# A decoder layer with a mixture of experts on one core: four whole expert tiles placed beside the cross attention's last chunk and the sort

## The chip, the cores and the metric

The kernel runs on one core of a Trainium2 chip. The metric is the time of one execution in device microseconds (us). Five engines work side by side, each through its own list of instructions in order: TensorE (PE; PEld is its weight load), VectorE (DVE), ScalarE (ACT), GpSimd (POOL) and SyncE (SP), which here only issues transfers. An instruction waits on semaphores for what it needs, and everything behind it on its engine waits with it.

## The reference, cut to what matters

`x` holds 2 x 1024 tokens of 256 numbers. Three blocks follow each other, each on a normalized copy of `x`, each added to `x`:

```python
x = x + self_attention(layernorm(x))         # 16 heads of 16, softmax plus a bias, then a layernorm
x = x + cross_attention(layernorm(x), ctx)   # 16 heads, 77 context tokens, masked
x = x + moe(layernorm(x))

def moe(flat):                               # 2048 tokens, 8 experts, hidden size 1024
    probs = softmax(flat @ gate_W)
    topk_w, topk_idx = top_k(probs, 2)       # every token goes to two experts
    combine = one_hot(topk_idx) weighted by topk_w / sum(topk_w)
    out = 0.5 * gelu(flat @ shared_W + shared_b)
    for e in range(8):
        h = gelu(flat @ W1[e] + b1[e])
        out = out + combine[:, e] * (h @ W2[e] + b2[e])
    return layernorm(out) * gamma + beta
```

Everything is float32. The kernel computes the experts only for the tokens that chose them: 4096 pairs of a token and an expert, sorted by expert.

## The kernel before, in words

The tokens are worked on in chunks of 512 (four chunks, `c` = 0 to 3) or in tiles of 128 (`i` = 0 to 15). `xs` holds `x`, 128 tokens by 16 tiles by 256. Up to some 475 us the self attention runs as a stream of products of scores (L549, L595), a maximum on VectorE (L556), an exponential on ScalarE (L603) and products with the values (L612).

From there until the sort is done, the order on PE, DVE, ACT and POOL is written out by hand: the string `todo` (L1124 to L1158) is a list of words, and each word calls one function, which issues its instructions on their engines in that order. The words for one tile of the cross attention are:

- `scores` (L681, PE: four products into four PSUM banks), `masked` (DVE: L696 four times, then the maximum L700), `less` (POOL, L705: subtracts the maximum, 128x1232), `exps` (ACT, L708), `sums` (DVE: L712 and L713), `shares` (POOL, L718: times the reciprocal, 128x1232);
- `turn` (L720: 16 transposes on PE, four copies on ACT into `PT`), and for each chunk `attend` (L731, two words) and `output` (L748, two words: products on PE, and L761 on DVE adds to `xs`).

After `output` a chunk is normalized for the experts: `stats` and `dev` (`measure`, and `norm_scale` at L134: L137 adds eps on DVE, L138 takes the power -0.5 on POOL), `off` (`offsets`, L167: L173 on DVE; the norm ahead of the cross attention multiplies by `live` first, L171), `norm` (four activations at L184, then the rows are written to `xnd` in DRAM), `flip` (transposes into `xnT`), `gate` (logits). `shared` are the products of the shared layer.

The sort follows when the gates are there, in three groups (chunks 0 and 1; 2; 3): `choose` takes the two best experts by a dozen small operations on DVE, `rank` counts on PE how many earlier pairs have the same expert, `place` makes slot numbers, `hots` (L881, L888) and `invert` (PE) turn the list around, `filled` adds the groups' parts. When all four chunks are in, `totals` and `owners` find for every tile of pairs its expert, `pick` and `rows` give for every slot the row to be gathered (`from_row`) and the row to be scattered to (`to_row`), and `biases` takes the tiles' biases.

An expert tile is then either 256 pairs (the first `NP` = 12) or 128 pairs (11 in this run). For each: POOL gathers its rows from `xnd` (L1466, an indirect transfer), PE transposes them (L1482) and DVE copies them into `xgT` (L1490), PE multiplies by the expert's first matrix (L1496), ACT applies gelu (L1503), PE multiplies by the second matrix (L1515), DVE adds the bias (`y`, L1522), POOL scatters `y` to `pairs` in DRAM (L1526). The weights, 1 MB for each of the two matrices, come by SP (L1384, L1389) into four sets of buffers, three tiles ahead. The order of this part is made by a scheduler. A last stage sums each token's two rows with the shared layer, normalizes and writes out.

Of the kernel before, what the change touches and what calls it, by code (L numbers as in the profile page):

```python
# [8 lines left out]
F32 = mybir.dt.float32  # L9
# [5 lines left out]
P = 128  # L15
# [18 lines left out]
NTE = NP + NS - 2 * NP  # L34
EB = N // P
# [5 lines left out]
def decoder_kernel(  # L41
# [92 lines left out]
    def norm_scale(mv, n, eps):  # L134

        r = small.tile([P, 4], F32, tag="rstd", name="rstd")
        nc.vector.tensor_scalar(r[:, :n], mv[:, :, 1], eps, None, ALU.add)  # L137
        nc.gpsimd.tensor_tensor(r[:, :n], r[:, :n], nhalf[:, :n], ALU.pow)  # L138
        return r
# [27 lines left out]
    def offsets(c, live=None, dst=None):  # L167

        mv, r = moments.pop(c)[1], tokens[c]
        if live is not None:  # L170
            nc.vector.tensor_tensor(r[:, :4], r[:, :4], live, ALU.mult)  # L171
        off = small.tile([P, 4], F32, tag="off", name=f"off{c}")
        nc.vector.scalar_tensor_tensor(off, mv[:, :, 0], -1.0, r[:, :4], ALU.mult, ALU.mult)  # L173
        if dst is None:
            dst = work.tile([P, 4, D], F32, tag="xn", name="xn")
        tokens[c] = r, off, dst
# [74 lines left out]
    for _ in range(30):  # L251
        nc.tensor.matmul(idle[:, :P], lhsT=ident, rhs=ident, start=True, stop=True)  # L252
# [406 lines left out]
    PTs, oTs = {}, {}  # L659
# [60 lines left out]
    def turn(i):  # L720
        c, t = i // 4, i % 4
        if c not in PTs:
            PTs[c] = cr2.tile([P, H, 512], F32, tag="PT", name=f"PT{c}")
        st = sts[i % 4]
        for k in range(4):
            pp = one("ppT").rearrange("p (h f) -> p h f", f=P)
            for h in range(4):
                nc.tensor.transpose(pp[:T2, h, :], st[:, 4 * k + h, :], ident)  # L728
            nc.scalar.copy(PTs[c][:T2, 4 * k : 4 * k + 4, P * t : P * t + P], pp[:T2, :, :])  # L729

    def attend(c, G):  # L731
        b, PT = c // 2, PTs[c]
        if c not in oTs:
            oTs[c] = cr2.tile([P, 2, 512], F32, tag="oT", name=f"oT{c}")
        po = one("pco")
        for i in range(2):
            for r in range(4):
                h = 8 * G + 2 * r + i
                nc.tensor.matmul(
                    po[32 * r : 32 * r + 32, :],  # L740
                    lhsT=vx[:T2, b, h, :, :].rearrange("p i d -> p (i d)"),
                    rhs=PT[:T2, h, :],
                    start=(i == 0),
                    stop=(i == 1),
                )
        nc.scalar.copy(oTs[c][:, G, :], po)

    def output(c, u):  # L748

        pu = one("pu").rearrange("p (t f) -> p t f", f=D)  # L750
        for t in range(2):
            for G in range(2):
                nc.tensor.matmul(
                    pu[:, t, :],
                    lhsT=oTs[c][:, G, P * (2 * u + t) : P * (2 * u + t) + P],
# [4 lines left out]
        x2 = xs[:, 4 * c + 2 * u : 4 * c + 2 * u + 2, :]  # L760
# [320 lines left out]
    def o_gamma(h):  # L1081
        c, o = out_of(h)
        mv = moments.pop(("o", c))[1]
# [12 lines left out]
    def exps_b(m):  # L1096
# [29 lines left out]
        exps_b:122 times_v:121:1 collect:14 exps_b:123 times_v:122:1 o_stats:14  # L1126
        exps_b:124 times_v:123:0 scores:0 o_dev:14 exps_b:125 masked:0 times_v:124:0
        exps_b:126 times_v:125:0 exps_b:127 times_v:126:0 o_gamma:14 scores:1 masked:1
        less:1 scores:2 masked:2 o_add:14 times_v:127:0 less:0 collect:15 exps:1
        q_stats:2 q_dev:2 o_stats:15 exps:0 o_dev:15 sums:0 o_gamma:15 q_off:2 less:2  # L1130
        sums:1 exps:2 o_add:15 sums:2 shares:0 q_norm:2 q_stats:3 close shares:1
        q_flip:2:1 add_bu:2 shares:2 scores:3 masked:3 q_flip:2:0 turn:0 less:3 scores:4
        q_dev:3 exps:3 masked:4 turn:1 sums:3 less:4 shares:3 scores:5 exps:4 masked:5
        turn:2 sums:4 query:2:1 query:2:0 less:5 shares:4 constant:0 scores:6 exps:5
        masked:6 turn:3 sums:5 less:6 shares:5 constant:1 scores:7 exps:6 attend:0:0
        masked:7 attend:0:1 turn:4 sums:6 q_off:3 less:7 shares:6 constant:2 scores:8
        q_norm:3 exps:7 masked:8 output:0:1 stats:0:1 output:0:0 q_flip:3:1 add_bu:3
        turn:5 sums:7 less:8 shares:7 constant:3 scores:9 q_flip:3:0 exps:8 masked:9
        turn:6 sums:8 less:9 shares:8 constant:4 scores:10 query:3:0 exps:9 masked:10
        query:3:1 turn:7 sums:9 less:10 shares:9 constant:5 scores:11 stats:0:0 exps:10  # L1140
        attend:1:0 masked:11 dev:0 attend:1:1 turn:8 sums:10 off:0 less:11 norm:0
        shares:10 constant:6 scores:12 exps:11 masked:12 output:1:1 stats:1:1 output:1:0
        turn:9 sums:11 less:12 shares:11 constant:7 scores:13 exps:12 masked:13
        flip:0:1:0 flip:0:0:0 turn:10 sums:12 gate:0 less:13 shares:12 constant:8
        scores:14 exps:13 masked:14 turn:11 sums:13 less:14 shares:13 constant:9
        scores:15 stats:1:0 exps:14 attend:2:0 masked:15 dev:1 attend:2:1 turn:12
        sums:14 off:1 less:15 norm:1 shares:14 exps:15 output:2:1 output:2:0 turn:13
        sums:15 shares:15 stats:2:1 flip:1:1:0 stats:2:0 flip:1:0:0 turn:14 dev:2 gate:1
        choose:0 earlier:1 turn:15 attend:3:0 attend:3:1 off:2 rank:0 place:0 output:3:0
        stats:3:0 output:3:1 norm:2 stats:3:1 dev:3 flip:2:1:0 flip:2:0:0 shared:0:0  # L1150
        hots:0:0 off:3 hots:1:0 norm:3 gate:2 hots:0:1 flip:3:1:1 choose:1 flip:3:0:0
        shared:1:1 gate:3 shared:3:0 rank:1 earlier:2 invert:0 choose:2 place:1 hots:2:0
        rank:2 hots:2:1 totals shared:3:1 hots:1:1 invert:1 place:2 hots:3:0 shared:0:1
        hots:3:1 filled:0 invert:3 owners invert:2 shared:2:0 filled:1 weights filled:2
        filled:3 pick shared:2:1 rows biases shared:1:0
# [34 lines left out]

    constants = []
# [10 lines left out]
    def zeros():  # L1202
        nc.gpsimd.memset(euler, 2.718281828459045)
        for t in (nta, ntb, twos, share2):
# [8 lines left out]
    slot_no = number("slot_no", [[1, NS]], 0, 0, [P, NS])  # L1213

    pair_no = number("pair_no", [[N, 2], [P, NT]], 2 * N, 1, [P, 2, NT])
    constants += [lambda: nc.gpsimd.memset(ones, 1.0), triangle, zeros]

    crossing = ExitStack()
    cr2 = crossing.enter_context(tc.tile_pool(name="cr2", bufs=2))
    cr1 = crossing.enter_context(tc.tile_pool(name="cr1", bufs=2))  # L1220
# [3 lines left out]
    filled_to = rt.tile([P, E, EB], F32, name="filled_to")  # L1224
# [22 lines left out]
    def owners():  # L1247
        nc.vector.tensor_tensor(
            filled_to,
# [7 lines left out]
        nc.vector.tensor_scalar(spare[:, 1, :], nta[:, 0, 4:], -1.0, float(EB), ALU.mult, ALU.add)  # L1257
        src, dst = nta, ntb
        for k in (1, 2, 4):
# [7 lines left out]
            twos[:, 1:], src[:, 1, 4:], 2.0, float(2 * NP), ALU.mult, ALU.min  # L1267
# [4 lines left out]
        for ts, to, no in (  # L1272
            (slice(0, NP), twos[:, 1:], slot_no[:, 0 : 2 * NP : 2]),
# [9 lines left out]
        nc.vector.tensor_reduce(owner, past, AX.X, ALU.add)  # L1283
        nc.vector.tensor_scalar(owner, owner, float(E - 1), None, ALU.min)
        nc.vector.tensor_copy(owner_i, owner)


        nc.vector.tensor_scalar(
            spare[:, 0, :], share2[:, :E], -1.0, float(EB), ALU.mult, ALU.add
        )  # L1290
        nc.vector.tensor_tensor(spare[:, 1, :], spare[:, 1, :], share2[:, 1:], ALU.add)
        for k, ts in enumerate((slice(0, NP), slice(NP, NTE))):
# [6 lines left out]
        nc.vector.tensor_reduce(skipped, over, AX.X, ALU.add)  # L1299
        nc.vector.tensor_tensor(  # L1300
            column[:, : 2 * NP].rearrange("p (i k) -> p i k", k=2),
            slot_no[:, : 2 * NP].rearrange("p (i k) -> p i k", k=2),
            skipped[:, :NP].unsqueeze(2).to_broadcast([P, NP, 2]),
# [3 lines left out]
            column[:, 2 * NP :], slot_no[:, : NTE - NP], share2[:, 0:1], skipped[:, NP:],  # L1307
            ALU.add, ALU.add,
        )
        nc.vector.tensor_scalar(pick, column, row_no[:, 0:1], None, ALU.is_equal)  # L1310
        nc.vector.tensor_copy(count_i, ends[:, E - 1 : E])

    def pick_columns():
        held["ppk"] = one("ppk")[:, :NS]
        nc.tensor.matmul(held["ppk"], lhsT=places, rhs=pick, start=True, stop=True)

    def rows():

        nc.vector.tensor_copy(pair, held["ppk"])
        nc.vector.tensor_scalar(from_row, pair, N - 1, None, ALU.bitwise_and)  # L1320
        nc.vector.tensor_scalar(to_row, pair, 2 * N, None, ALU.bitwise_xor)

    def biases():

        nc.vector.tensor_scalar(mine, owner[:E, :], row_no[:E, 0:1], None, ALU.is_equal)
        pb1 = one("pb1")[:, : NTE * NH].rearrange("p (i h) -> p i h", h=NH)
        for h in range(NH):
            nc.tensor.matmul(
                pb1[:, :, h], lhsT=b1[:, h * P : (h + 1) * P], rhs=mine, start=True, stop=True
            )  # L1330
        nc.vector.tensor_copy(b1s, pb1)
# [22 lines left out]
        pick=pick_columns,  # L1354
        rows=rows,
        biases=biases,
# [9 lines left out]
    w1s = [wmoe.tile([P, 2, HID], F32, name=f"w1_{k}") for k in range(3)]  # L1366
# [371 lines left out]
```

## Time and profile before

| | us |
|---|---|
| median of 3 runs (977.98 to 978.78) | 978.05 |
| the profiled execution's own time | 986.99 |
| its span, first to last instruction | 985.3 |
| self attention's last products with values end (PE) | 501.8 |
| tile 15's `sums` (L712) begin | 609.2 |
| first gather of expert rows begins (POOL) | 668.8 |
| first products of an expert begin (PE, L1496) | 676.3 |
| first expert tile's `y` (L1522) | 700.7 |
| last stage's first sums (L1615) | 955.1 |

In the windows of the profile each column behind an engine's busy time is its number of instructions; PEclk is the clock that TensorE was granted, 1.00 being full speed. A busy PE is an upper bound: its products are pipelined and their ends are modelled, so the spacing of the starts tells more than the sum of durations. In the timeline a row gives start, duration, engine, line, what is written from what, and in brackets the idle time before it and what ended it.

### The profile page before, as it was taken

The numbers are of one execution on the slowest core, as the hardware profiler recorded it, in microseconds if no ns is written. First come the engines' busy times: TensorE is split into PE (matmuls) and PEld (weight loads), VectorE is DVE, ScalarE is ACT, GpSimd is POOL, SyncE is SP. The second block draws the span as 40 slices with busy tenths as digits, with TensorE's granted clock in tenths as the row PEclk, the third lists the DMA queues.
The fourth block names the chain that finished last, engine by engine and source line by source line (L and its number), as shares of the span: only waits on it lengthen the run. The fifth ranks groups of instructions, "written<-read, shape, count | busy, mean of one in ns | idle before, by whom it ended". The sixth has DMA issues, their size and how long they took to land.

```text
span 985.3 us, 16174 instructions
## 1 busy us (share of the span) xinstructions
PE 922.7 (94%) x6080; PEld 542.9 (55%) x6080; DVE 579.4 (59%) x1172; ACT 544.1 (55%) x1079; POOL 403.5 (41%) x344
## 2 busy tenths in 40 slices
PE   9999999999999999999947999998999999999983
PEld 6543433333333333333315667686878878888762
DVE  5874668878888797987589998471111031011117
ACT  4566767877878788887844777313332322234312
POOL 1642323553335564343566887005243432122103
PEclk9999999999999999999976999689999999999997
DMA  7300000000000000000000000007854654699343
GB/s 172 59 1 2 2 2 1 2 1 1 2 1 2 1 2 1 1 1 1 1 0 18 1 23 22 27 17 264 307 196 156 206 180 153 206 308 329 132 145 125
DMA packets 65162, 75.62 MB, mean 77 GB/s; under 512 B 17967, under 2 KB 57036, under 8 KB 65076
## 3 DMA queue, kind: packets, MB, share of 16 engines
q1 hardware_dynamic: 59604, 63.62, 20.0%
q0 software_dynamic: 3360, 8.79, 2.4%
q10 hardware_dynamic: 2112, 2.10, 0.6%
q8 instruction: 50, 0.82, 0.4%
q14 instruction: 36, 0.29, 0.1%
HBM read 66.10 MB, written 8.78 MB: 76 GB/s over the span
## 4 chain that ended last, share of the span: by engine, by line
PE 72%; DVE 15%; DMA 9%; issue 2%; ACT 1%; POOL 1%; SPq 0%; DVEq 0%; POOLq 0%; ACTq 0%
PE sA L549 14%; PE av L612 13%; PE sB L595 11%; PE po L1515 9%; PE ph L1496 9%; DMA pairs<-y,to_row 7%; PE pp L502 3%; PE pb L394 2%; PE pv L340 1%; DVE cm L700 1%; DVE cs L712 1%; PE pq L664 1%; DVE scrap L696 1%; PE idle L252 1%; DVE xs L1094 1%
## 5 line engine op out<-in xcount | busy, mean ns | idle before, releaser
L556 DVE TENSOR_REDUCE mx<-sA 128x1 f32<-128x512 f32 x512 | 317.4, 683 | 95.4 <-PE sB L595 88.4
L603 ACT ACTIVATE pt<-sB 128x512 f32<-128x512 f32 x512 | 264.8, 603 | 63.1 <-PE sB L595 63.0
L549 PE MATMUL sA<-kT,scrap 32*128 32x512 f32 x1024 | 253.8, 619 | 0.0
L595 PE MATMUL sB<-qB,kT 32*128 32x512 f32 x1024 | 247.6, 616 | 0.0
L625 POOL TENSOR_TENSOR avs<-avs,part 128x512 f32<-128x512 f32 x112 | 142.1, 1269 | 231.0 <-ACT part L624 225.7
L1503 ACT ACTIVATE hT<-ph,b1s 128x256 f32<-128x256 f32 (+1 forms) x184 | 77.7, 424 | 184.6 <-PE ph L1496 179.7
L549 PEld LDWEIGHTS sA<-kT,scrap 32*128 32x128 f32 x1024 | 100.4, 183 | 82.3 <-ACT pt L603 54.5
L612 PE MATMUL av<-pt,vaug 128*32 128x512 f32 x1024 | 137.4, 605 | 3.2 <-DVE mx L556 3.2
L595 PEld LDWEIGHTS sB<-qB,kT 32*128 32x128 f32 x1024 | 97.7, 183 | 37.9 <-issue 30.1
L1522 DVE TENSOR_TENSOR y<-po,b 128x512 f32<-128x512 f32 (+1 forms) x23 | 13.0, 564 | 176.4 <-PE po L1515 169.7
L1496 PE MATMUL ph<-xgT,w 128*128 128x256 f32 (+1 forms) x576 | 109.3, 334 | 1.3 <-DMA w<-in_L_ffn_W_dram 0.7
L1515 PE MATMUL po<-w,hT 128*128 128x256 f32 x432 | 105.2, 382 | 3.4 <-DVE y L1522 3.3
L1496 PEld LDWEIGHTS ph<-xgT,w 128*128 128x128 f32 x576 | 91.3, 191 | 21.4 <-ACT hT L1503 7.5
L1515 PEld LDWEIGHTS po<-w,hT 128*128 128x128 f32 x432 | 77.7, 190 | 14.4 <-DVE y L1522 5.5
L1526 POOL DMA_INDIRECT pairs<-y,to_row x35 | 35.3, 1007 | 115.1 <-DMA pairs<-y,to_row 79.4
L1466 POOL DMA_INDIRECT xg<-xnd,from_row x35 | 34.3, 979 | 104.5 <-PE px L1482 64.2
L612 PEld LDWEIGHTS av<-pt,vaug 128*32 128x32 f32 x1024 | 21.0, 109 | 100.4 <-DVE mx L556 91.4
L624 ACT COPY part<-av 128x512 f32<-128x512 f32 x108 | 65.7, 609 | 5.4 <-PE av L612 5.1
L138 POOL TENSOR_TENSOR rstd<-rstd,nhalf 128x4 f32<-128x4 f32 x20 | 21.7, 1084 | 71.2 <-DVE rstd L137 70.8
L729 ACT COPY PT<-ppT 77x512 f32<-77x512 f32 x64 | 32.7, 588 | 2.2 <-PE ppT L728 1.5
L1515 PE MATMUL po<-xnT,hT 128*128 128x256 f32 x128 | 31.8, 383 | 1.9 <-DVE y L1522 1.9
L194 PE MATMUL pxT<-ident,xn 128*128 128x128 f32 x96 | 17.5, 305 | 16.7 <-ACT xn L184 16.6
(262 smaller groups left out, 1137.9 us busy)
## 6 DMA issues: line engine op xcount, KB each, us to landing
w<-in_L_ffn_W_dram SPq DMA_DIRECT2D x36, 1024.0 KB
xnT<-in_L_ffn_W_dram SPq DMA_DIRECT2D x10, 1024.0 KB
b<-in_L_ffn_b_dram SPq DMA_DIRECT2D x23, 128.0 KB
xs<-in_x_dram SPq DMA_DIRECT2D x4, 512.0 KB
xnd<-xn SPq DMA_DIRECT2D x4, 512.0 KB
w<-pairs SPq DMA_DIRECT2D x3, 512.0 KB
w<-pairs ACTq DMA_DIRECT2D x3, 512.0 KB
out_dram<-scrap SPq DMA_DIRECT2D x3, 512.0 KB
```

What stands on the lines that cost most here:

```text
L549: nc.tensor.matmul(s, lhsT=units[h // 4, "q"][r0 : r0 + 32, q0 : q0 + P], rhs=units[h // 4, "k", g % 2][r0 : r0 + 32, 512 * kh : 512 * kh ...
L556: nc.vector.tensor_reduce(largest[h][:, qt, hh : hh + 1, kh], s, AX.X, ALU.max)
L595: nc.tensor.matmul(s, lhsT=units[h // 4, "k", g % 2][r0 : r0 + 32, kt * P : (kt + 1) * P], rhs=shifted[h][r0 : r0 + 32, :], start=True, st ...
L603: nc.scalar.activation(powers[m, hh], s, AF.Exp, scale=1.0 / 16.0)
L612: nc.tensor.matmul(av[32 * hh : 32 * hh + 32, :], lhsT=vaug[:, kt, 4 * g + hh, :, b], rhs=powers.pop((m, hh)), start=True, stop=True,)
L624: copy(part, av)
L625: nc.gpsimd.tensor_tensor(sums[h], sums[h], part, ALU.add)
L1466: fetched[i] = nc.gpsimd.indirect_dma_start(out=xg[:, s, :], out_offset=None, in_=xnd[:, :], in_offset=bass.IndirectOffsetOnAxis(ap=from_r ...
L1496: nc.tensor.matmul(ph[:, hc % group, :], lhsT=w1[:, kc, hc * P : (hc + 1) * P], rhs=xgT[:, kc, :], start=(kc == 0), stop=(kc == 1),)
L1503: hidden[i] = nc.scalar.activation(hT[:, hc, :], ph[:, hc % group, :], AF.Gelu, bias=b1s[:, i, hc : hc + 1])
L1515: nc.tensor.matmul(po[:, s, :], lhsT=hT[:, hc, s * P : (s + 1) * P], rhs=w2[:, hc, :], start=(hc == 0), stop=(hc == NH - 1),)
L1526: nc.gpsimd.indirect_dma_start(out=pairs[:, :], out_offset=bass.IndirectOffsetOnAxis(ap=to_row[:, k : k + 1], axis=0), in_=y[:, s, :], in_ ...
```

## The change: what it does, and the diff

Of the 12 tiles with 256 pairs, four (`NE`) are made out of the first three chunks alone. When group 1 is sorted, `counts` and `full` find four whole tiles among the experts' pairs so far, `pick_full`, `rows_full` and `biases_full` do for them what `pick`, `rows` and `biases` do for all, and `used` takes them off the later count. Their parts (`load`, `fetch`, `spread`, `first`, `second`) stand as words in `todo` beside the last chunk's words; eight tiles of 256 and the 11 of 128 remain for the loop. `first` is a quarter of the first layer, `second` half of the second. For this the sort's groups 0 and 1 are moved ahead, between the words of tiles 11 to 15. `turn`, `attend` and `output` work on pairs of tiles, 256 tokens, in place of chunks; the products and copies for a chunk stay the same in number of columns. The norm's addition of eps, the product with `live` and the offset (now two instructions) are issued on POOL. At the start 27 in place of 30 products keep PE busy. The weights of tiles 0 and 2 lie in half of `xnT` and a buffer of their own, those of 1 and 3 in the buffer of `PT`. SP's list, in the built order: the rows of chunks 0 to 2, the loads of tiles 0 and 1, the rows of chunk 3, the first matrix of tile 2, its second, the first matrix of tile 3, then some sixteen loads of owners into registers, and behind them the second matrix of tile 3 and the loads of tiles 4 and on.

```diff
     def norm_scale(mv, n, eps):
         r = small.tile([P, 4], F32, tag="rstd", name="rstd")
-        nc.vector.tensor_scalar(r[:, :n], mv[:, :, 1], eps, None, ALU.add)
+        nc.gpsimd.tensor_scalar(r[:, :n], mv[:, :, 1], eps, None, ALU.add)
         nc.gpsimd.tensor_tensor(r[:, :n], r[:, :n], nhalf[:, :n], ALU.pow)
...
         if live is not None:
-            nc.vector.tensor_tensor(r[:, :4], r[:, :4], live, ALU.mult)
+            nc.gpsimd.tensor_tensor(r[:, :4], r[:, :4], live, ALU.mult)
         off = small.tile([P, 4], F32, tag="off", name=f"off{c}")
-        nc.vector.scalar_tensor_tensor(off, mv[:, :, 0], -1.0, r[:, :4], ALU.mult, ALU.mult)
+        nc.gpsimd.tensor_tensor(off, mv[:, :, 0], r[:, :4], ALU.mult)
+        nc.gpsimd.tensor_scalar(off, off, -1.0, None, ALU.mult)
...
-    for _ in range(30):
+    for _ in range(27):
         nc.tensor.matmul(idle[:, :P], lhsT=ident, rhs=ident, start=True, stop=True)
...
     todo = """
...
+        gate:1 choose:0
+        turn:11 less:13 shares:12 scores:14 attend:5 exps:13 masked:14 sums:13 rank:0
+        place:0 output:5 earlier:1 stats:2:1 hots:1:0 turn:12 hots:0:1 less:14 shares:13
+        dev:2 scores:15 off:2 exps:14 shared:1:1 masked:15 sums:14 norm:2 shared:1:0
+        flip:2:1:0 flip:2:0:0 gate:2 shared:2:0 turn:13 hots:0:0 choose:1 less:15
+        shared:2:1 shares:14 rank:1 invert:0 earlier:2 exps:15 hots:1:1 sums:15 attend:6
+        counts filled:0 invert:1 place:1 hots:2:1 turn:14 hots:2:0 shares:15 invert:2
+        full shared:0:0 load:0 filled:1 filled:2 pick_full rows_full output:6 turn:15
+        biases_full attend:7 fetch:0 used fetch:1 spread:0 fetch:2 output:7 stats:3:0
+        stats:3:1 dev:3 load:1 first:0:0 off:3 norm:3 first:0:1 first:0:2 first:0:3
+        spread:1 fetch:3 flip:3:0:1 flip:3:1:0 first:1:0 first:1:1 second:0:0 second:0:1
+        load:2 gate:3 first:1:2 first:1:3 choose:2 spread:2 totals rank:2 place:2
+        hots:3:1 hots:3:0 first:2:0 second:1:0 shared:3:0 invert:3 owners first:2:1
+        filled:3 pick second:1:1 load:3 first:2:2 rows first:2:3 spread:3 second:2:0
+        first:3:0 biases first:3:1 first:3:2 first:3:3 second:3:0 weights second:2:1
+        second:3:1 shared:3:1
     """.split()
...
+    def full_tiles():
+        nc.vector.tensor_tensor(
+            full_to,
+            held["pce"].unsqueeze(2).to_broadcast([P, E, NFULL]),
+            bounds.unsqueeze(1).to_broadcast([P, E, NFULL]),
+            ALU.is_ge,
+        )
+        nc.vector.tensor_reduce(fta[:, 4:], full_to, AX.X, ALU.add)
+        src, dst = fta, ftb
+        for k in (1, 2, 4):
+            nc.vector.tensor_tensor(dst[:, 4:], src[:, 4:], src[:, 4 - k : 4 - k + E], ALU.add)
+            src, dst = dst, src
...
+    def set_of(i):
+        return i % 2 if i < NE else (i - NE + 2) % 4
...
+    def fetch_first(i):
+        for s in range(2):
+            gather(2 * i + s, xgs[i % 2], s, N - N // 4)
+
+    def turn_first(i):
+        px = one("px").rearrange("p (kc f) -> p kc f", kc=2)
+        for kc in range(2):
+            for s in range(2):
+                nc.tensor.transpose(
+                    px[:, kc, s * P : (s + 1) * P], xgs[i % 2][:, s, kc * P : (kc + 1) * P], ident
+                )
+        nc.vector.tensor_copy(xgTs[0], px)
+
+    def first_part(i, q):
+        ph = one("ph").rearrange("p (h f) -> p h f", h=2)
+        for j in range(2):
+            hc = 2 * q + j
+            for kc in range(2):
+                nc.tensor.matmul(
+                    ph[:, j, :],
+                    lhsT=weights[i][0][:, kc, hc * P : (hc + 1) * P],
+                    rhs=xgTs[0][:, kc, :],
+                    start=(kc == 0),
+                    stop=(kc == 1),
+                )
+            nc.scalar.activation(
+                hTs[i % 2][:, hc, :], ph[:, j, :], AF.Gelu, bias=b1s[:, i, hc : hc + 1]
+            )
+
+    def second_part(i, s):
+        w2, b2 = weights[i][1]
+        if s == 0:
+            held["po2", i] = one("po2").rearrange("p (s f) -> p s f", s=2)
+        po, y = held["po2", i], ys[i % 2]
+        for hc in range(NH):
+            nc.tensor.matmul(
...
+        if s == 0:
+            return
+        nc.vector.tensor_tensor(y, po, b2.unsqueeze(1).to_broadcast([P, 2, D]), ALU.add)
+        for s in range(2):
+            scatter(2 * i + s, y, s)
...
-        got = {0: fetch(0)}
-        gate_in = nc.sync.dma_start(out=landed, in_=xgs[0][0:1, :, 0:1])
-        got[1] = fetch(1)
+        got = {NE: fetch(NE)}
+        gate_in = nc.sync.dma_start(out=landed, in_=xgs[NE % 3][0:1, :, 0:1])
+        got[NE + 1] = fetch(NE + 1)
         with tc.issue_after(gate_in.ins):
-            second_of_0()
-            weights[1] = fetch_weights(1)
-            weights[2] = fetch_weights(2)
+            weights[NE + 1] = fetch_weights(NE + 1)
+            weights[NE + 2] = fetch_weights(NE + 2)
...
-        behind = tiles((0, 2), always + 2, got, None)
-        behind = tiles((2, always), always + 2, got, behind)
+        behind = tiles((NE, NE + 2), always + 2, got, None)
+        behind = tiles((NE + 2, always), always + 2, got, behind)
```

## The prediction

> **What bounds the kernel now.** I read the slices first.
>
> ```profile
> PE   9999999999999999999947999998999999999983
> DVE  5874668878888797987589998471111031011117
> POOL 1642323553335564343566887005243432122103
> PEclk9999999999999999999976999689999999999997
> ```
>
> One slice is 24.6 us. Up to slice 20 PE is full and DVE has room. In slices 20 to 25 DVE is full: cross attention. In 25 to 27 nobody is full and PE's clock drops: the sort. From 28 on PE is full and DVE idle: the expert tiles. So four tiles can be had for less than they cost only if they fill holes that DVE, or the low clock, makes in PE's time between 500 and 680 us. The windows of that stretch:
>
> ```profile
> 560.00:580.00 20.00, 19.19 (x133) 11.89 (x133) 19.59 (x35) 15.14 (x26) 17.71 (x15) 1.00 0.01 1
> 580.00:600.00 20.00, 20.00 (x152) 14.94 (x154) 19.59 (x37) 14.49 (x25) 17.04 (x12) 1.00 0.08 27
> ...
> 616.00:633.00 17.00, 17.00 (x68) 9.84 (x67) 4.73 (x20) 3.93 (x8) 0.00 (x0) 0.52 0.10 32
> ```
>
> After the window's length come PE, PEld, DVE, ACT and POOL, then the clock. DVE has 19.59 of 20 us, and POOL 17 to 18. In the third PE seems full, but at clock 0.52, with 68 products in 17 us. The timeline shows why DVE is full:
>
> ```profile
> 554.06 2.25 POOL L705 TENSOR_TENSOR st<-st,cm 128x1232 f32<-128x1232 f32 x1
> ...
> 555.08 1.25 DVE L171 TENSOR_TENSOR rstd<-rstd,live 128x4 f32<-128x4 f32 x1
> 556.26 2.25 POOL L718 TENSOR_TENSOR scrap<-scrap,cs 128x1232 f32<-128x1232 f32 x1
> 556.36 2.17 DVE L173 SCALAR_TENSOR_TENSOR off<-bnmv,rstd 128x4 f32<-128x4 f32 x1
> ```
>
> Operations on four columns, 0.15 us elsewhere, end just when POOL's product ends (556.31, 558.51): with SBUF inputs DVE waits for POOL. L700 and L712 keep their 1.43 us beside POOL. The chain of waits, too, goes mostly through DVE's L696, L700 and L712 from 499 to 609. Last, the loop's pace:
>
> ```profile
> 700.69 0.69 DVE L1522 TENSOR_TENSOR y<-po,b 128x512 f32<-128x512 f32 x1 [4.76 <-PE po L1515]
> ...
> 715.64 0.69 DVE L1522 TENSOR_TENSOR y<-po,b 128x512 f32<-128x512 f32 x1 [3.59 <-PE po L1515]
> ```
>
> A tile of 256 costs 14.95 us of the path, PE without holes.
>
> **The sum.** What follows the loop's first `y` is 985.3 - 700.7 = 284.6 us, and loses 4 x 14.95 = 59.8. So the change wins if that `y` comes less than 59.8 us later than 700.7. I build that time from two stretches.
>
> **Stretch one, paced by DVE,** from tile 1's `masked` (L696 at 498.9) until the early tiles' `from_row` is written. DVE's work in the new order, with before's rows:
> - 15 `masked` (1.53 + 1.44) and 16 `sums` (1.43 + 0.21): 44.6 + 26.2 = 70.8
> - two output norms (2.1 of statistics, L1085 2.74, L1094 4.09, waits for POOL included): 17.8
> - five chunk norms' statistics, 2.1 each: 10.5; six L761 of 0.66 and a `collect`: 4.7
> - the sort of groups 0 and 1: `choose` 3.1 + 2.6, `place` 1.6 + 1.4, six `hots` of 1.64 (0.68 + 4 x 0.27, overlapping), 9.8 in all, copies, `earlier` and `filled` 2.0, `full` 15 small operations at 0.2, 3.0, and rows 0.5: 24.0
>
> Together 127.8. Before did 97.9 of such work between 498.9 and the end of tile 15's `sums` (610.8), in 111.9 us: 14 us over. Of these L171 and L173 took 6.4 (1.25 + 2.17 + 1.81 + 1.80, less 4 x 0.16); they go, as the change puts them on POOL. The other 7.6 are waits for PE or ACT; I keep 7.
>
> New is that the sort's small operations with SBUF inputs stand between tiles 11 and 15, where POOL is busy. At five places (`choose:0`, `place:0`, `hots:1:0`, `hots:0:0`, `place:1`) a `shares` or `dev`/`off` has just become ready. Bounds: 0, if DVE slips in ahead, to 20 us, eight 2.25 us products of POOL left there and 2 us of a norm. I take 2.0 for each of the five, near the 1.25 to 2.17 of the rows above: 10. So 498.9 + 127.8 + 7 + 10 = **643.7**. PE's own work here, 112 us by the spacing of the rows (`scores` 1.24, `turn` 1.82, `attend` and `output` 1.8, `query` 1.75, `shared` and `gate` 1.85), fits beneath.
>
> The norms' 19 instructions on POOL in this stretch have no row. Bounds: 0.13 to 0.19 (IOTA, CAST of few columns) and 1.0 (L138, a power). I take 0.2, nearest in kind: 4 us among 94 of POOL's, in 145. That hides; at 1.0 it fits still, and only chunk 2's norm, on which group 1 waits, would come 3 us later. They read statistics from DVE as L137 and L173 did, and ACT's L184 waits behind them, as before. At the kernel's end two L137 of 1.25 and 1.19 us vanish from DVE, but the addition then queues behind the same product on POOL: 0, between 0 and -2.
>
> **Stretch two, paced by PE.** After `from_row` PE still has `output` 1.8, `turn` 1.9, the biases 2.0, `attend` 1.8, the transposes 0.6, `output` 1.8 = 9.9. That covers the gather: before, 5.7 us from from_row's last operation (667.9) to L1482 (673.6). It covers the first weights: the owner is known some 2 us before 643.7, its register load took 1.2 (owner_i written at 664.3, load issued at 665.4), and 1 MB with another ahead 9.1 (677.35 to 686.5): 652. First expert product: 653.6. From there four tiles and the last chunk: first layers 4 x 7.1, second 4 x 7.0, three transposes 1.8, `flip` 1.1, `gate` 1.85, `totals` 1.4, `rank` 1.3, two `shared` 3.8, `invert` 2.0, `pick` 0.4, biases 2.0 = 72.0, so 725.6. DVE has only some 25 us of work in this stretch; chunk 3's sort waits for PE, not the reverse. Then the loop: transposes and copy 1.6, two first layers 14.2, one second 7.0: 748.4.
>
> Hops between engines: 3.5 us (seven turns of `spread` or of gelu before a product, 0.5 each, as L1522 to L1515's 0.35 or L1503's 0.39). Clock: before ran 27 us of 606 to 681 at about half, costing some 13.7 us of PE; bounds 0 and 13.7. I take two stretches of 3.4 us, the length of the three short drops, 3.4 lost, because PE is fuller: **755.3**. The scatters of two tiles (7 us apart each) fall into stretch two on POOL; nothing on PE waits for them before `y` of the loop's second tile, 15 us later. Three idle products fewer at the start (0.16 us each, two instructions per product, 1.0): the transposes follow at 11.12 but their input is ready at 10.35; gain 0.6.
>
> Sum: 755.3 - 700.7 - 59.8 - 0.6 = **-5.8 us** against the profiled run, 986.99 to 981.2. The runs shown have a median 978.05, 8.9 below it; the difference carried over gives 972.2.
>
> The Trainium skill speaks against one piece: "SBUF — State Buffer", in "A bandwidth-pool intuition that's wrong", says that a transfer issued by GpSimd waits for its descriptors while DVE holds the shared port, some 620 ns becoming some 3100. No row before shows it: L1466 took 0.95 to 1.22 us with DVE nearly idle, and in the changed kernel gathers run beside the sort. By that rule the first tile's two gathers would come an estimated 5 us later, and the sum would be near -1.
>
> **Rivals.**
> 1. *Everything fits* (0.20): DVE is let in ahead of POOL (-7), no clock drop (-3.4), hops hidden (-2): -18, 960. For it: PE's holes close as work fills them. Against: waits in every stretch of the trace.
> 2. *DVE shut out by POOL* (0.26), slower: place, group 0 and 1's sort among tiles 11 to 15; price up to 10 us more, and while PE waits for `taken` and `place` its clock falls, which costs up to 10 more. It decides once `from_row` comes 6.4 us later than 643.7, after 650.1. Likeliest 11 us over, +5: 983, at most 992. For it: 0.52 of the clock in exactly these words before. That the holes aren't there at all, PE being "9" in the slices, ends here too.
> 3. *Late weights* (0.09): the second matrix of tile 3 waits behind some sixteen register loads on SP after `owners`. Between 0 and the 1.2 us above for each, up to 19 us, with some 20 us of PE work over it; 6 us may show: 978, no change.
> 4. *Forecast* (0.45).
>
> **Numbers.** 972.2. Range 960 to 986: rival 1's value below, most of rival 2 above; about 2 in 10 stay out. One measurement tells 0.2%, 2 us, from no change. Faster 0.65 (forecast and rival 1), same 0.09, slower 0.26.
>
> **What would show it.** `from_row` of the early tiles near 644, first L1496-like product near 654, first `y` of the loop near 755, then 14.95 us a tile. In the words around `choose` and `hots`, DVE operations whose ends match POOL's ends, some 2 us at five places. PEclk at 0.5 for two stretches only between 600 and 690. Wrong if `from_row` comes after 650, if PE waits for weights, or if a POOL instruction of four columns takes 1 us.

## The result, and the profile after

The changed kernel takes 1005.03 us (median of 4 runs, 1001.54 to 1008.06) against 978.41 of the kernel before beside it: a ratio of 1.0262, interval 1.0217 to 1.0306. It is slower by 26.6 us, where 5.8 us less were predicted. Its profiled execution took 1003.7 us with a span of 1002.0.

The slices of the changed kernel (one is 25.05 us), to lay beside those of before:

```profile
PE   9999999999999999999929998978999999989973
DVE  5774668877887887968598888612301141011107
POOL 2732323553345664443477974211214431145104
PEclk9999999999999999999969997969999999999997
```

Counted from 0, as in the prediction: DVE is less full in slices 20 to 24 (9, 8, 8, 8, 8 for 8, 9, 9, 9, 8), and the first expert products now stand in slice 26. But there PE has 7 and its clock 6, and in slice 27 PE has 8: holes, where before's expert tiles ran at 9 (from slice 28 on). The windows there (window's length, PE, PEld, DVE, ACT, POOL, clock, DMA share, GB/s):

```profile
650.00:660.00 10.00, 8.48 (x56) 6.13 (x56) 3.87 (x15) 2.49 (x4) 2.34 (x3) 0.83 1.05 350
660.00:670.00 10.00, 5.39 (x14) 3.61 (x13) 0.12 (x1) 3.70 (x8) 1.73 (x4) 0.68 0.29 101
670.00:680.00 10.00, 8.87 (x31) 6.72 (x30) 1.38 (x2) 2.48 (x5) 2.05 (x2) 0.64 0.35 114
```

Between 660 and 670 PE issues 14 rows of products (against 56 in the window before), and neither DVE, ACT, POOL nor the DMA is busy for more than 3.7 of the 10 us: they wait for each other. The timeline of PE shows for what (start, duration, line, in brackets the idle time before it):

```profile
657.09 1.03 PE L1503 MATMUL ph<-xgT,xnT 128*128 128x256 f32 x4
658.68 1.99 PE L1503 MATMUL ph<-xgT,xnT 128*128 128x256 f32 x8 [0.56 <-ACT hT L1510]
664.72 3.78 PE L1503 MATMUL ph<-xgT,xnT 128*128 128x256 f32 x8 [4.04 <-ACT hT L1510]
669.06 3.78 PE L1503 MATMUL ph<-xgT,xnT 128*128 128x256 f32 x8 [0.56 <-ACT hT L1510]
673.41 2.08 PE L1503 MATMUL ph<-xgT,xnT 128*128 128x256 f32 x4 [0.56 <-ACT hT L1510]
```

Four rows of products make one group, and a part is two groups, for two blocks of 128 hidden columns. After every first group PE stands 0.56 to 0.62 us until ACT's gelu (L1510) has read it. Once it stands 4.04 us, and then eight rows take 3.78 us instead of 1.99: half the clock. ACT's own row for the 4.04 is `norm:3`, four scalings that wait for POOL's offset and have the next gelu behind them:

```profile
662.23 2.07 ACT L189 ACTIVATE xn<-xs,off,rstd 128x256 f32<-128x256 f32 x4 [1.91 <-POOL off L178]
664.21 0.45 ACT L1510 ACTIVATE hT<-ph,b1s 128x256 f32<-128x256 f32 x1
```

The waits of PE between 650 and 775 us (in total, times, longest) put nearly all of it in one line, and no wait for weights is among them (the 0.6 put down to "issue" stands at the same place of a part, 727.5, so it is probably the sixteenth wait of this kind):

```profile
PE ph L1503 <- ACT hT L1510: 12.4, 15, 4.0
PE px L1493 <- DMA xg<-xnd,from_row: 1.0, 2, 0.6
PE px L1662 <- ACT scrap L929: 0.7, 1, 0.7
PE ph L1503 <- issue: 0.6, 1, 0.6
PE ph L1676 <- DVE xgT L1670: 0.4, 1, 0.4
```

Set against the prediction's marks: the early tiles' `from_row` is written at 645.0 (predicted 643.7; the row is below), the first expert product is at 657.1 (653.6), the loop's first `y` at 775.4 (755.3). Then the loop keeps its pace, 14.95 us a tile:

```profile
644.98 0.17 DVE L1424 TENSOR_SCALAR from_row<-pair 128x8 int32<-128x8 int32 x1
775.35 0.69 DVE L1702 TENSOR_TENSOR y<-po,b 128x512 f32<-128x512 f32 x1 [4.76 <-PE po L1695]
790.31 0.69 DVE L1702 TENSOR_TENSOR y<-po,b 128x512 f32<-128x512 f32 x1 [3.84 <-PE po L1695]
```

From that `y` to the end it is 226.6 us (predicted 224.8). So 20.1 of the lost time lies before the loop's first `y`, and nearly all of it after `from_row`.

### The profile page after: what moved, and what is told of

It is laid out like the page before. It is cut to its first block, busy times and chain, and to the rows that moved or that the text cites. A ratio compares the mean times of both kernels' runs of the same rounds, so it can differ in the third digit from the quotient of the medians.

```text
span 1002.0 us, 16525 instructions
## 1 busy us (share of the span) xinstructions
PE 926.3 (92%) x6222; PEld 548.4 (55%) x6222; DVE 573.6 (57%) x1159; ACT 543.1 (54%) x1079; POOL 415.3 (41%) x400
## 4 chain that ended last, share of the span: by engine, by line
PE 66%; DMA 10%; DVE 9%; issue 8%; POOL 4%; ACT 2%; POOLq 0%; DVEq 0%; ACTq 0%; SPq 0%
PE sA L554 14%; PE av L617 13%; PE sB L600 11%; DMA pairs<-y,to_row 9%; PE ph L1503 4%; PE po L1520 3%; PE pp L507 3%; PE ppT L731 2%; PE sC L686 2%; PE pb L399 1%; PE pq L669 1%; PE pu L760 1%; PE pxT L199 1%; PE ph L1676 1%; POOL pairs L1476 1%
## 5 line engine op out<-in xcount | busy, mean ns | idle before, releaser
L1683 ACT ACTIVATE hT<-ph,b1s 128x128 f32<-128x128 f32 (+1 forms) x152 | 62.6, 412 | 142.5 <-PE ph L1676 136.4
L1702 DVE TENSOR_TENSOR y<-po,b 128x256 f32<-128x256 f32 (+1 forms) x19 | 10.2, 537 | 133.1 <-PE po L1695 125.0
L1695 PE MATMUL po<-w,hT 128*128 128x256 f32 x336 | 83.2, 382 | 2.4 <-DVE y L1702 2.3
L1695 PEld LDWEIGHTS po<-w,hT 128*128 128x128 f32 x336 | 59.7, 190 | 10.3 <-DVE y L1702 3.7
L1676 PE MATMUL ph<-xgT,xnT 128*128 128x128 f32 (+1 forms) x320 | 57.2, 320 | 0.0
L1676 PEld LDWEIGHTS ph<-xgT,xnT 128*128 128x128 f32 x320 | 49.0, 190 | 9.4 <-ACT hT L1683 3.5
L1510 ACT ACTIVATE hT<-ph,b1s 128x256 f32<-128x256 f32 x32 | 15.1, 473 | 59.0 <-PE ph L1503 54.7
L731 PE MATMUL ppT<-ident,scrap 128*77 128x128 f32 x192 | 26.2, 295 | 16.3 <-POOL scrap L723 13.4
L731 PEld LDWEIGHTS ppT<-ident,scrap 128*77 128x77 f32 x192 | 24.3, 163 | 19.3 <-POOL scrap L723 13.6
L507 PE MATMUL pp<-xnT,scrap 128*128 128x512 f32 x64 | 31.2, 613 | 0.4 <-DVE xnT L202 0.4
```

What stands on the lines that cost most here:

```text
L507: nc.tensor.matmul(pp, lhsT=wqk[name][:, kc, P * G : P * G + P], rhs=xnT[:, kc, b * S + 512 * j : b * S + 512 * j + 512], start=(kc == 0), ...
L731: nc.tensor.transpose(pp[:T2, h, :], st[:, 4 * q + h, :], ident)
L1676: nc.tensor.matmul(ph[:, hc % group, :], lhsT=w1[:, kc, hc * P : (hc + 1) * P], rhs=xgT[:, kc, :], start=(kc == 0), stop=(kc == 1),)
L1683: hidden[i] = nc.scalar.activation(hT[:, hc, :], ph[:, hc % group, :], AF.Gelu, bias=b1s[:, i, hc : hc + 1])
L1695: nc.tensor.matmul(po[:, s, :], lhsT=hT[:, hc, s * P : (s + 1) * P], rhs=w2[:, hc, :], start=(hc == 0), stop=(hc == NH - 1),)
```

## The experiments

Theory A: in the early tiles PE waits for a gelu in the middle of every part, because both halves lie in one PSUM tile; the waits and the low clock that follows them are the loss. Rival B: the early tiles are held up by data (weights, gathered rows) or by DVE standing still beside POOL. Rival C: the low clock comes whatever PE waits for. Rival D: POOL's small operations delay the norms. Each time is a median beside runs of the kernel before on the same chip (medians of 979.5 to 979.8); the ratio is to that kernel, with its interval.

**Gelus behind both groups.**

```diff
 def first_part(i, q):
     for j in range(2):
         ...matmul(ph[:, j, :], ...)
-        nc.scalar.activation(hTs[i % 2][:, hc, :], ph[:, j, :], AF.Gelu, ...)
+    for j in range(2):
+        nc.scalar.activation(hTs[i % 2][:, hc, :], ph[:, j, :], AF.Gelu, ...)
```

> The changed kernel with one edit: a part of an early tile's first layer issues its two groups of products first and its two gelus behind them, where the changed kernel put the first gelu between the groups. Theory A (PE waits 0.56 us for the gelu of the first group before it may write the other half of the same PSUM tile, fifteen times in the trace, and its clock stays low for it): 15 x 0.56 = 8.4 us go, and 2 to 5 us of low clock with them; 1005.0 becomes 992 to 995, and the row 'ph waits for hT' falls from 12.4 us to under 5, the 4.0 us one remaining. Rival B (the early tiles are slow because weights and rows come late, or DVE stands still beside POOL): no change, 1003 to 1007. Rival C (the low clock has a fixed number of stretches, whatever PE waits for): only the 8.4 us, 996 to 997, with the same low stretches between 660 and 690.

Measured: 979.04 us, ratio 0.9986 (0.9960 to 1.0012). All 26 us are gone, twice what A expected. The profile says why it is more. The first layer of tile 0 is one row now, and all parts of all tiles follow without a wait; between 660 and 690 the clock stays at 1.00:

```profile
659.03 7.07 PE L1503 MATMUL ph<-xgT,xnT 128*128 128x256 f32 x32
665.93 0.60 PE L1493 MATMUL px<-ident,xg 128*128 128x128 f32 x4
```

```profile
660.00:670.00 10.00, 10.00 (x53) 8.78 (x52) 3.20 (x10) 6.21 (x15) 3.79 (x6) 1.00 0.48 158
670.00:680.00 10.00, 10.00 (x55) 9.01 (x54) 0.99 (x3) 1.03 (x3) 1.03 (x1) 1.00 0.32 124
```

The place of `norm:3` no longer matters either: PE runs ahead into other PSUM tiles while ACT is held. The loop's first `y` comes at 751.6, and from 660 to 760 no window is below 1.00; the one from 650 to 660 has 0.66:

```profile
650.00:660.00 10.00, 8.63 (x57) 6.12 (x58) 2.07 (x8) 1.87 (x2) 2.84 (x3) 0.66 0.96 346
751.59 0.69 DVE L1704 TENSOR_TENSOR y<-po,b 128x512 f32<-128x512 f32 x1 [4.76 <-PE po L1697]
```

B and C fall.

**The norm of chunk 3 later.**

```diff
-first:0:0 off:3 norm:3 first:0:1 first:0:2 first:0:3
+first:0:0 off:3 first:0:1 first:0:2 first:0:3 norm:3
```

> The changed kernel with one word moved: the norm of chunk 3 on ACT (four scalings that wait for POOL's offsets) stands behind the four parts of the first early tile's first layer instead of between the first and second. Theory A (ACT, in order, held the gelus behind a wait for POOL; PE stood 4.0 us, and then ran at half clock from 664.7 to about 677, which lost some 5 us): 4 us and 3 to 6 us of clock go, 995 to 998. Rival B (PE has nothing else to do there and the wait only moves to the transposes of chunk 3): 1003 to 1006. Rival C (the clock falls anyway): only the 4 us, 1001.

Measured: 997.06 us, ratio 1.0163 (1.0096 to 1.0230): 8 us less than the changed kernel, as A expected. The hole of 4.0 us is gone and the clock is 1.00 from 660 to 720 (0.60 from 720 to 730); the other waits stay, now at an even beat, which gives their price:

```profile
658.52 1.99 PE L1503 MATMUL ph<-xgT,xnT 128*128 128x256 f32 x8 [0.56 <-ACT hT L1510]
661.08 1.99 PE L1503 MATMUL ph<-xgT,xnT 128*128 128x256 f32 x8 [0.56 <-ACT hT L1510]
663.64 1.99 PE L1503 MATMUL ph<-xgT,xnT 128*128 128x256 f32 x8 [0.56 <-ACT hT L1510]
666.20 1.13 PE L1503 MATMUL ph<-xgT,xnT 128*128 128x256 f32 x4 [0.56 <-ACT hT L1510]
```

A part every 2.56 us, against 6.90 / 4 = 1.73 in the run above: a wait shown as 0.56 us costs 0.83. Some 0.16 of the difference is the modelled end, which reaches into the gap (a row shows 0.38 us, while rows without a wait follow each other every 0.22), and 0.10 is a slower start: four rows behind a wait take 1.13 us instead of 1.03.

**Both edits.**

> The changed kernel with both edits: gelus behind both groups of products in each part, and the norm of chunk 3 behind the first tile's first layer. Theory A: the two add up, 12.4 us of waits and 4 to 8 us of low clock go: 985 to 989, first y of the loop at about 758 in place of 775.4. Rival B: 1003 to 1006. Even under A it stays 7 us or more over the kernel before, since from_row, the gather and the blocks ahead of the first expert product are untouched.

Measured: 981.93 us, ratio 0.9988 (0.9952 to 1.0024); not to be told from the first edit alone. The expected 985 to 989 was too high, and "the two add up" was wrong: once PE needs no gelu inside a part, the norm's place only shifts a wait of 1 us to chunk 3's transposes.

**The gelus where they were, the two groups in two PSUM tiles.**

```diff
+    if q % 2 == 0:
+        for j in range(2):
+            held["ph", j] = one("ph").rearrange("p (h f) -> p h f", h=2)
...
-        ...matmul(ph[:, j, :], ...)
+        ph = held["ph", j][:, q % 2, :]
+        ...matmul(ph, ...)
```

> The changed kernel with the gelus left between the two groups of products as they were, but the two groups written to two different PSUM tiles (two parts share two tiles crosswise, so that as many are used). Theory A (the wait comes from one PSUM tile that PE writes while ACT reads its other half): the waits go as in gelu_after, 976 to 982. Rival B (what helped gelu_after was the order on ACT or PE and not the shared tile): 1002 to 1007, with waits of 0.56 us still between the groups.

Measured: 980.93 us, ratio 0.9996 (0.9962 to 1.0031). The order of the instructions is that of the changed kernel; only the tile differs, and the time is back. So the wait belongs to the shared PSUM tile, which here is one PSUM bank. One wait of the early tiles is left, the one that `norm:3` makes:

```profile
657.57 5.34 PE L1506 MATMUL ph<-xgT,xnT 128*128 128x256 f32 x24
665.92 2.52 PE L1506 MATMUL ph<-xgT,xnT 128*128 128x256 f32 x8 [3.00 <-ACT hT L1513]
```

**Idle products in the waits.** The changed kernel, with four idle products between the two groups of each part of tiles 0 and 1.

```diff
+            if j == 0 and i < 2:
+                fill = one("fill")
+                for _ in range(4):
+                    nc.tensor.matmul(fill[:, :P], lhsT=ident, rhs=ident, start=True, stop=True)
             nc.scalar.activation(...)
```

> The changed kernel with four idle products of 128 x 128 (about 0.6 us) on PE between the two groups of each part of early tiles 0 and 1: extra work that changes no result and puts no wait away, but keeps PE busy in eight of the sixteen waits. Theory A (waits cost twice: 0.83 us each in the spacing of the products, and the low clock that gaps keep going, 664.7 to 677 and later): the low clock in 660 to 690 goes, some 4 to 6 us, and 1005 becomes 998 to 1002. Rival C (the clock falls for other reasons than gaps): 1004 to 1008, as low a clock as before.

Measured: 1002.41 us, ratio 1.0215 (1.0139 to 1.0290); the interval overlaps that of the changed kernel, so the time decides nothing. The clock does: 0.83, 0.83, 1.00 in the three windows from 650 to 680, where the changed kernel had 0.83, 0.68, 0.64.

```profile
660.00:670.00 10.00, 6.91 (x33) 6.06 (x32) 0.04 (x1) 3.69 (x8) 1.74 (x4) 0.83 0.41 145
670.00:680.00 10.00, 10.00 (x65) 9.10 (x64) 1.29 (x2) 3.91 (x8) 2.05 (x2) 1.00 0.37 133
```

There is still a drop around the hole (it stays, 3.09 us), but with the small gaps filled the clock comes back after it. The later drops, in the tiles that have no filler, are gone too in this execution; with one trace of each kernel none of this is proof.

**Two early tiles instead of four** (with the first edit).

```diff
-NE = 4
+NE = 2
```

The words of tiles 2 and 3 (`load`, `fetch`, `spread`, `first`, `second`) leave the list.

> The kernel gelu_after with two early tiles instead of four (the other two go to the loop). If PE, once the gelu waits are gone, has no holes left between 659 and 740 (as its windows show), an early tile of the last two fills nothing: 976 to 982, the same as gelu_after (979.0). If the early tiles 2 and 3 do fill waits of the last chunk's sort: 983 to 990, with low clock between 690 and 730. If they cost more there than in the loop (hops, shorter rows): 970 to 975.

Measured: 989.70 us, ratio 1.0096 (1.0065 to 1.0127), 10.7 us over four tiles: the second of the three expectations. The last chunk's sort does open holes, and tiles 2 and 3 fill them:

```profile
690.00:700.00 10.00, 6.10 (x38) 5.15 (x36) 4.60 (x25) 0.03 (x1) 0.97 (x2) 1.00 0.63 219
700.00:710.00 10.00, 7.16 (x31) 5.56 (x31) 1.75 (x3) 0.95 (x2) 7.75 (x8) 0.79 0.50 158
```

With four tiles PE has 10.00 in both. So early tiles do fill holes, as the change meant them to; they have to earn the price of a sort done twice first.

**Only the norms' small work on POOL**, in the kernel before: the addition of eps, the product with `live` and the offsets, as the change has them.

```diff
-        nc.vector.tensor_scalar(r[:, :n], mv[:, :, 1], eps, None, ALU.add)
+        nc.gpsimd.tensor_scalar(r[:, :n], mv[:, :, 1], eps, None, ALU.add)
...
```

> The kernel before with only the norms' small work on POOL (addition of eps, product with live, offsets in two instructions): the change's third part alone. The prediction's step: 6.4 us of DVE's time in cross attention go, POOL's small operations hide; so between 972 and 978. Rival D (POOL's small operations, measured at 0.22 to 0.47 us and queued behind products of 2.25 us, delay each norm and so the sort and the end): slower than before, 980 to 984. If the norms lie off the path: 977 to 979.

Measured: 975.93 us, ratio 0.9956 (0.9920 to 0.9992): 3.8 us faster, inside the range expected; D falls. The mended change of the first experiment holds this part too and took 979.04: its early tiles and everything else it brings are not shown to gain anything on top of the norms, and by the medians cost some 3 us (the intervals of the two ratios overlap). In its trace the loop's first `y` is at 687.6:

```profile
L1523 DVE TENSOR_TENSOR y<-po,b x23: 423/691/692, 687.6 to 932.5; 128x512 f32<-128x512 f32 x12, 128x256 f32<-128x256 f32 x11
```

**The kernel before, a second profile,** with nothing edited.

> The kernel before, unchanged, for a second profile: the first was of an execution of 986.99 us, 8.9 over the median, and the prediction carried these 8.9 over to the changed kernel. If they are low clock in the sort (27 us at about half between 606 and 681), an execution near 978 shows 10 to 20 us of it less, and its first y of the loop near 692 instead of 700.7, while its loop and last stage take the same 284.6 us; the difference is then no constant of the program, and nothing to carry over. If the 8.9 lie elsewhere (start, loop, end), first y is at 700 and the rest shorter.

Measured: 980.94 us, and its rows of `y`:

```profile
692.00 0.69 DVE L1522 TENSOR_TENSOR y<-po,b 128x512 f32<-128x512 f32 x1 [4.76 <-PE po L1515]
706.96 0.69 DVE L1522 TENSOR_TENSOR y<-po,b 128x512 f32<-128x512 f32 x1 [3.81 <-PE po L1515]
```

First `y` at 692.0 where the prediction read 700.7; from there 287.2 us instead of 284.6. The clock of 600 to 640 was 0.96 here and 0.77 there:

```profile
600.00:640.00 40.00, 37.92 (x265) 31.91 (x258) 28.02 (x90) 22.18 (x42) 11.49 (x12) 0.96 0.12 40
```

The first profile of before had caught an execution with a long stretch of low clock in the sort. Of the 65 executions of this kernel timed beside the experiments, 55 took 977.2 to 982.2 us and ten 986.3 to 989.9; the 986.99 that the prediction started from is of the rarer kind.

**A better order.** The first edit, and two words moved in the sort of group 2, where DVE stood 1.0 and 2.3 us.

```diff
-flip:2:0:0 gate:2 shared:2:0 turn:13 hots:0:0 choose:1 less:15 shared:2:1 shares:14 rank:1
+flip:2:0:0 hots:0:0 gate:2 shared:2:0 turn:13 choose:1 less:15 shares:14 rank:1
...
-shares:15 invert:2 full
+shares:15 shared:2:1 invert:2 full
```

> The kernel gelu_after with two pieces of the sort of group 2 moved in the written order: hots:0:0 on DVE ahead of gate:2 (DVE stood 1.0 us there, waiting for the gate's products), and shared:2:1 on PE from before rank:1 to before invert:2 (DVE stood 2.3 us there, since earlier:2 waits for rank:1's products; PE itself has a hole of 1.4 us before invert:2). If from_row is set by that chain through DVE, it comes 1.7 to 2.7 us sooner than 645.7, and the whole 976 to 978 in place of 979.0 to 980. If PE from 645 on is what counts (its work there is only moved), 979 to 981.

Measured: 976.52 us, ratio 0.9977 (0.9963 to 0.9990). This version beats both kernels: by 0.23% the one before, and the changed one by 2.8% (0.9977 / 1.0262 = 0.972). It stands beside the norms alone (0.9956): between those two the intervals overlap.

**Eleven idle products in PE's holes**, on top of that order.

```diff
+    def warm(n):
+        spare_ps = one("warm")
+        for _ in range(n):
+            nc.tensor.matmul(spare_ps[:, :P], lhsT=ident, rhs=ident, start=True, stop=True)
...
-rank:0 ... gate:2 ... pick_full
+warm:5 rank:0 ... warm:3 gate:2 ... warm:3 pick_full
```

> order_one with eleven idle products of 128 x 128 (0.22 us each) on PE, where it stood waiting: five ahead of rank:0 (a hole of 1.3 us), three ahead of gate:2 (0.7) and three ahead of pick_full (0.7). Theory A (gaps of PE bring the low clock 3 to 7 us later): the drops at 606 to 610, 616 to 627 and 650 to 657 shrink, some 5 to 7 us at full clock are won on a path that goes through gate:2 and the first early tile: 970 to 974. Rival C (the clock does not follow such short gaps): as order_one or up to 1.5 us more, 977 to 980.

Measured: 977.94 us, ratio 0.9977 (0.9959 to 0.9996): no gain. The clock answers in part (1.00 in the window 600 to 610 for 0.72 in order_one, 0.97 for 0.66 from 620 to 630, but 0.86 for 0.93 between them), while the time before `from_row` is set by DVE: PE now waits 2.4 us for `taken` where it waited 1.3 and computed slowly, and `from_row` comes 0.7 us sooner (643.8 against 644.5). The drop at 650 to 660 is deeper (0.66 for 0.83). Theory A's half on the clock holds in part, its half on the time does not.

## Why the prediction was wrong, point by point

**The step that failed** is stretch two's "hops between engines: 3.5 us (seven turns of `spread` or of gelu before a product, 0.5 each)", on top of first layers at 7.1 us each. The 7.1 was read from the loop's rows. The loop's source has the same products, gelu, products, gelu, but its scheduler lets the groups go in turn to two PSUM tiles, as the fourth experiment does by hand; a product still has to follow a gelu, with a group of the other tile in between, and 32 rows run in 7.07 to 7.19 us. The early tiles' order is written out: both groups of a part into one PSUM tile with the gelu between them. The diff of `first_part` showed this, and the built order has a wait for ACT before each second half; I counted the turns between words and not the waits inside one. The sum of what the runs show, from `from_row` to the loop's first `y`, the changed kernel (130.4 us) against the first experiment (105.9):

- fifteen waits at 0.83: 12.5 us;
- the one of 4.0 us, beyond its share above: 3.5;
- the clock: by the windows from 650 to 760, 23.8 us at half in the changed kernel (0.83, 0.68, 0.64, 0.83, 0.83) and 6.8 in the experiment (0.66). Half of the difference is 8.5.

Together 24.5, and 24.5 were measured. That they agree to the tenth is luck: the third term is an estimate, as some low-clock time fell into waits, and a sixteenth wait would add 0.8.

**The clock**, "two stretches of 3.4 us, 3.4 lost, because PE is fuller": as predicted where PE is full (6.8 us at half in the first experiment), and off by 8.5 where it is not. I treated hops and clock as two terms; without the waits the drops behind 660 went as well. That the small gaps alone bring the clock down is not shown: with them in place the second experiment had 1.00 from 660 to 720, and 0.60 from 720 to 730. The sign "PEclk at 0.5 for two stretches only between 600 and 690" failed in either kernel: by the 10 us windows 27 us were at half in the changed kernel and 20 in the first experiment, 10 and 14 of them before 640, where DVE sets the pace and `from_row` was in time all the same.

**"The difference carried over gives 972.2"** failed as well. The 8.9 us between the profiled run of before and its median were low clock in one execution. They sat in the stretch that the change rebuilds, and in the runs of the changed kernel there is no such difference (1003.7 against a median of 1005.03). Without the waits the prediction's own sum, 981.2 for a profiled run, meets the 980.97 that the first experiment's profiled run took, and its `y` at 755.3 the 751.6 there; that the totals meet to 0.2 is partly luck, as `y` came 3.7 us sooner and the rest took 227.6 us for 224.8. Against a common execution of before (first `y` at 692.0) that is a gain of 692.0 + 59.8 - 751.6 = 0.2 us: nothing. So even with the mechanism right, "-5.8" was measured from an uncommon execution.

**Right:** `from_row` at 645.0 for 643.7. Of the five places of 2 us where DVE waits beside POOL, the changed kernel shows three: L819 (2.17), L873 (1.78) and L863 (2.20). The loop's pace of 14.95, with no wait of PE on the early tiles' scatters in its first four tiles. POOL's small operations took 0.25 to 0.33 us on average for the 0.2 taken, L142 1.05 as before, and hid.

**The rivals.** "DVE shut out by POOL" named 983 to 992 and the point 650.1 for `from_row`; at 645.0 it did not decide. "Late weights": no wait for them on PE. Slower came by a fourth way that I had not listed, and of the three signs that would have shown the forecast wrong none appeared (only L142, the power, took 1 us, and it did so before).

**Gathers, the shared bank and the clock.** The prediction set the Trainium skill's page "SBUF — State Buffer" against the change. In the changed kernel the gathers' issues took 0.94 to 1.23 us, as before, and from the start of `from_row` to the first transposes of gathered rows it was 7.6 us instead of 6.0. By the page it would have been an estimated 5 us more. But the first four were issued between 645.5 and 650.4, where DVE had 0.8 us of work, so the rule was hardly put to the test. Weights came in at the same time (350 GB/s from 650 to 660), and what took the 1.6 us was not tried. Two other pages of the Trainium skill were the ones to read. "PSUM — Partial Sum Buffer", in "PSUM bank collisions raise a hardware error", says that TensorE must not write a bank while another engine reads it, whatever the columns, and that semaphores are to guard PSUM by bank and quadrant or, more simply, by bank. The rows fit a wait of this kind: 0.56 us shown, 0.83 us of beat, and gone with a second bank. Whether the bank asks for it or only the tile is not shown, since an early `ph` is both. "TensorE: Matmul & The Clock Gate", in Part 1, gives windows of some 3.4 us in which the clock is decided by activity; the clocks of 10 us windows above, 0.83 and 0.66, are one and two such pieces at half.

**What stays open.** Products by pairs were not tried alone. The price of sorting twice is known only as a difference: with two early tiles the loop's first `y`, less two tiles' pace (731.4 - 29.9 = 701.5), is 9.5 us later than in a common execution of before, and that holds everything else the change does as well. What starts and ends each drop of the clock was not isolated.

## What to carry to other kernels

When work moves from a loop that a scheduler orders into an order written by hand, price it by the waits in its own instruction list and not by the loop's rows; two groups of products in one PSUM tile of one bank, with a reader between them, were a wait each time here. Put the readers behind all writers of the tile, or let the groups alternate between two. And before a profile serves as the base of a sum, ask whether it shows a common execution: a difference between the profiled run and the median belongs to a place in the trace, and goes if that place is rebuilt.

## What the runs showed of the hardware that was not expected

A gap of PE that the profile shows as 0.56 us cost 0.83 us in the spacing of products, half as much again. And one gap of 4.0 us, with small gaps of 0.56 every 4.3 us behind it, went with a clock at half for some 12 us (664.7 to 677), while a hole of 3.1 us at the same place, with those gaps filled by idle products, went with one short drop. In these two traces, one execution of each kernel, small gaps seem to have kept a low clock low; they did not bring a full one down between 660 and 720 in the second experiment.
